# A two-layer decoder on one core: three single routed tiles share one buffer of three rows, with an empty step before their transposes, and three bias operations move behind Layer 0's last block

## The chip, the cores and the metric

The kernel runs on one core of a Trainium2 chip. The metric is the device time of one execution, in microseconds (us); the times given are the median of several runs. Beside them there is one profiled execution of each kernel, with a trace of every instruction; all line numbers (L208 and so on) are those of the kernel before, in its profile.

The engines are called TensorE (PE in the profile; PEld is its loading of weights), VectorE (DVE), ScalarE (ACT), GpSimd (POOL) and SyncE (SP). Each takes its instructions in the order of its own queue.

## The reference

Two decoder layers over x of shape (32, 100, 256), that is 3200 tokens of 256 numbers, with a context of shape (32, 361, 128). Cut to what matters:

```
x = x + L0_attn(layernorm(x))            # causal softmax attention, 16 heads of 64
x = x + L0_xattn(layernorm(x), ctx)      # cross attention to the context
x = x + L0_ffn(layernorm(x))             # 8 experts, top 2, and a shared expert
x = x + L1_attn(layernorm(x), W1, b1, W2, b2)   # linear attention scores, causal mask, 16 heads of 16
x = x + L1_xattn(layernorm(x), ctx)      # softmax cross attention, 16 heads of 64
x = x + L1_ffn(layernorm(x))             # 64 experts, top 8 in 4 of 8 groups, and a shared expert
```

The routing of the last stage, for each token:

```
scores = sigmoid(x @ gate_weight.T)
sfc = scores + e_bias
group_scores = sum of the two largest sfc in each of 8 groups of 8
keep the 4 best groups, then the 8 best experts of those
weights = scores of these 8, divided by their sum, times 2.5
expert e takes its tokens in order, at most 256
```

Everything is float32. The bias b1 of Layer 1's attention goes to the queries, the keys and the values.

## The kernel before

**Tiles and batches.** The 3200 tokens lie in SBUF as 25 tiles of 128 tokens (`x_sb`), numbered 0 to 24. Attention works by batches of 100 tokens, numbered 0 to 31, so a tile is complete when the batch that holds its last token is done. `tile_of(b)` says which tile batch b completes. Tiles 21, 22, 23 and 24 are completed by batches 28, 29, 30 and 31, one each.

**Who sets the order.** TensorE's order is written out by hand (`manual_schedule`): it follows the program. The other engines' orders are made by a scheduler, which takes operations as their inputs are expected to be ready, unless a dependency is added by hand (`self.depend`). A buffer with a tag rotates: with `bufs=2`, the third use waits until the first one's readers are done.

**Layer 0's experts.** `blocks0_run` runs 29 blocks in the order `ORDER0`: 24 of 256 rows and five of 128 rows ("half blocks"). In each, `block0` multiplies by the two hidden matrices (L155), ScalarE makes the silu (L1340) and VectorE the product `h` (L1341); then come the transposes of the next block's rows (L1299) and the products with the third matrix (L1362, L1368), which VectorE copies out (L1374). That copy is `self.late`. Behind each block, `behind` issues some of the small loads of Layer 1's weights and biases from a list (L1248), four of the small ones for a block; among them sixteen for the query biases (`wB<-in_bq`) and sixteen for the key biases (`wB<-in_bk`). Each block's own weights come by an indirect DMA of GpSimd (L1277).

**Layer 1's biases.** `l1_attn` puts three small operations on VectorE: two at L942 spread the query biases over two columns, and one at L943 copies the key biases. Their result `bias` is read by ScalarE when it evacuates queries and keys (L973, L970). In front of Layer 1's attention, L1266 adds the gathered expert rows to `x_sb`.

**Layer 1's cross attention with the routing beside it.** In `l1_xattn`, each batch has 13 steps. A step holds, on TensorE, the scores of one group of 128 query rows (L155), often one further matmul group, such as a part of the next batch's values projection (`vals1`), and the three transposes of an earlier group (L784). ScalarE makes the exponentials (L775, `wBx`) and copies the transposes (L785, `eT`); VectorE makes the maxima (L772) and scales the rows (L777). At the fourth step the values of the batch before are multiplied (L796).

When a tile is complete, `out` adds the projection to `x_sb` (L808 and L812) and takes the statistics for the norm. Its square root runs on ScalarE (L202), the reciprocal on VectorE (L205). The table `ROUTED` says which tiles are routed together: groups of three from tile 0 to 20, and then tiles 21, 22, 23 and 24 singly. `route` is a generator: at each `yield` it ends its part of the current step, and `tick` takes every open route on by one part at the end of each step. Its parts are: the normalised rows `xr` (L208), the transposes by TensorE (L230, evacuated by L149 or L150 in turn into `xnT`), the gate matmuls with the sigmoid (L1595), the choice of groups and experts on VectorE (L1598 to L1661), the places of the tokens with their experts (two matmuls, L1667 to L1677, giving `slot`), and eight sends for each tile: indirect DMAs of GpSimd (L1682), each of which writes 128 rows of `xr` to DRAM. There is at most one send in a step, and each waits for a piece of work of its step.

A row of `xr` is the 256 normalised numbers, the token's number (copied in by GpSimd, L1582) and 64 weights. Groups of three use the tag `xr`, with two buffers of three rows. Single tiles use the tag `xn`, with two buffers of two rows, of which one row is used:

```
if G == RG:
    xr = rp.tile([P, RG, XROW], F32, tag="xr", name="xr", bufs=2)
else:
    xr = self.lnp.tile([P, 2, XROW], F32, tag="xn", name="xr2")[:, :G]
```

**The end.** The last batch's steps, and the last tile's route, have parts of the shared expert between them (`shared1`, L1828, L1829 and L1836). When all sends have landed, GpSimd sets a flag, SyncE loads the first experts' rows, and `units` runs the experts of Layer 1, adding their results by indirect DMAs.

Of the kernel before, what the change touches and what calls it, by code (L numbers as in the profile page):

```python
# [9 lines left out]
F32 = mybir.dt.float32  # L10
# [3 lines left out]
ALU = mybir.AluOpType  # L14
AX = mybir.AxisListType

P = 128
# [3 lines left out]
NF = NT // P  # L21
# [23 lines left out]
XROW = D + 1 + E1  # L45

HALVES = {0: 6, 6: 6, 12: 6, 18: 7}
EDGES = {0: 6, 6: 6, 12: 6, 18: 3, 21: 2, 23: 2}
ROUTED = {**{f: 3 for f in range(0, 21, 3)}, **{f: 1 for f in range(21, NF)}}
FRONT0 = {**{f: 4 for f in range(0, 20, 4)}, 20: 5}  # L50
FRONT1 = {0: 4, **{f: 3 for f in range(4, NF, 3)}}
RG = 3
# [46 lines left out]
class Kernel:  # L99
# [619 lines left out]
    def l1_xattn(self):  # L719
        nc, tc, a = self.nc, self.tc, self.a  # L720
        self.route_begin()
        with ExitStack() as st:
# [80 lines left out]
            def out(f, part):  # L803
# [8 lines left out]
                nc.vector.tensor_tensor(self.x[:, f, :], self.po, self.x[:, f, :], ALU.add)  # L812
                self.norm_stats(f, ROUTED)
                for f0, n in ROUTED.items():
                    if f0 + n == f + 1 < NF:
# [105 lines left out]
    def l1_attn(self):  # L921
        nc, tc, a = self.nc, self.tc, self.a
        with ExitStack() as st:
            self.psum = st.enter_context(self.banks("l1a", t=8))
            wk, wq, wv, wo, bqk, bv, bo, xbo = self.w1a
# [11 lines left out]
            own = cp.tile([P, 2], F32, tag="own", name="own")  # L937
            nc.vector.tensor_single_scalar(own[:, 0:1], at, 0.0, op=ALU.is_equal)
            nc.vector.tensor_single_scalar(own[:, 1:2], at, 16.0, op=ALU.is_equal)
            bias = cp.tile([P, 3, 2], F32, tag="bias", name="bias")  # L940
            for j in range(2):
                nc.vector.tensor_scalar(bias[:, j, :], bqk[:, 0, :], own[:, j : j + 1], None, ALU.mult)  # L942
            nc.vector.tensor_copy(bias[:, 2, :], bqk[:, 2, :])  # L943
            vs = [cp.tile([T, H, 32], F32, tag=f"v{i}", name=f"v{i}") for i in range(3)]
            for v in vs:
                nc.gpsimd.memset(v, 0.0)
# [3 lines left out]
            def group(i):  # L950

                f = (0, 3 * i + 1)[i > 0]
                return range(f, f + FRONT1[f])
# [99 lines left out]
            with tc.manual_schedule(engines={mybir.EngineType.PE}):  # L1053
                for i in range(2):
# [9 lines left out]
                    f = group(i)[0]  # L1064
# [6 lines left out]
                for b in range(NB + 2):  # L1071
                    i = b % 4
# [497 lines left out]
    def route(self, f, G):  # L1570


        nc, tc, rp = self.nc, self.tc, self.rp
# [1 line left out]
        def t3(name, *shape, dt=F32):  # L1575
            return rp.tile([P, RG, *shape], dt, tag=name, name=name)[:, :G]

        if G == RG:
            xr = rp.tile([P, RG, XROW], F32, tag="xr", name="xr", bufs=2)
        else:  # L1580
            xr = self.lnp.tile([P, 2, XROW], F32, tag="xn", name="xr2")[:, :G]
        nc.gpsimd.tensor_copy(xr.bitcast(I32)[:, :, D], self.tok[:, f : f + G])  # L1582
        for j in range(G):
            self.norm_row(f + j, xr[:, j, :D], nc.vector)
            if j % 2 or j == G - 1:
                yield 1
        for j in range(0, G, 2):
            n = min(2, G - j)
            self.norm_turn(f + j, n, xr[:, j : j + n, :D], self.bank_t())
            yield 1  # L1590
# [88 lines left out]
        for j in range(G):  # L1679
            for k in range(TOPK):  # L1680
                yield SEND
                got = nc.gpsimd.indirect_dma_start(  # L1682
                    out=self.x1_d[:, :],
                    out_offset=bass.IndirectOffsetOnAxis(ap=slot[:, j, k : k + 1], axis=0),
                    in_=xr[:, j, :], in_offset=None,
                    bounds_check=E1 * CAP - 1, oob_is_err=False,
                )
# [63 lines left out]
    def l1_ffn(self):  # L1751
        nc, tc, a = self.nc, self.tc, self.a
        x = self.x
        with ExitStack() as st:
# [6 lines left out]
            with tc.manual_schedule(engines={mybir.EngineType.PE}):  # L1761
                next(steps)
                next(steps)

                (used, _), = self.routes
                next(used)
                next(route)
                us = next(steps)
                next(used)
                next(route)  # L1770
                us += next(steps)
                next(used)
                for _ in route:
                    pass
                while us < FIRST1:
                    us += next(steps)
# [309 lines left out]
```

## Time and profile before

| What | us |
|---|---|
| median of 3 runs | 2970.16 (2968.84 to 2970.37) |
| the profiled execution | 2999.12 |
| its span, first to last instruction | 2997.4 |
| TensorE busy in it | 2866.1 (96%) |
| VectorE busy | 1789.8 (60%) |
| ScalarE busy | 1415.9 (47%) |
| GpSimd busy | 914.0 (30%) |
| mean granted TensorE clock | 0.981 of full speed |
| Layer 0's blocks of experts | from about 1183 to 1592 |
| the last three batches' steps and values | from about 2684 to 2791 |
| the first load of experts' rows issued | 2830.9 |

The profiled execution is 1% longer than the median of the runs. A profile line of a group of instructions names line, engine, operation, output and inputs; brackets give the idle time of the engine just before it, and what ended that. The granted clock is a share of full speed: at 0.5 a matmul takes twice as long.

### The profile page before, as it was taken

To read this page: it belongs to the slowest core of one execution; us is meant where nothing else is said; L and a number is where in the kernel's file an instruction comes from. 1 tells how busy PE (TensorE), PEld (TensorE's weight loads), DVE (VectorE), ACT (ScalarE), POOL (GpSimd) and SP (SyncE) were. 2 spreads that over 40 slices of the span, in tenths; PEclk is the share of its full clock that TensorE was granted. 3 is DMA by queue.
4 is the path that set the end of the run, shared out by engine and by line. 5 is a ranking of instruction groups with operands and counts; after the bars stand their busy time and mean duration, and the time that the engine had idled before them with its cause. 6 is when DMAs were issued, how large, how long until landed. Compare 5 with 4: busy or idle time off the path is not lost. (4 is left out here: it accounts for less than half of the span.)

```text
span 2997.4 us, 66479 instructions
## 1 busy us (share of the span) xinstructions
PE 2866.1 (96%) x26012; PEld 2176.5 (73%) x26012; DVE 1789.8 (60%) x5120; ACT 1415.9 (47%) x4261; POOL 914.0 (30%) x1040
## 2 busy tenths in 40 slices
PE   8999999999999999999998999999999999998993
PEld 7777777677777756888885667777777777775672
DVE  6665666577777742222225778676666676776454
ACT  5554555567666631221223224565566566566220
POOL 3222221266655544100005431021311212123364
PEclk9999999999999989999998999999999999999997
DMA  9870000000000023654552100010000000000297
GB/s 316 272 276 1 1 1 1 14 15 16 15 15 15 8 87 122 211 202 183 199 217 74 32 2 10 6 42 20 26 11 12 12 12 11 12 10 5 83 229 194
DMA packets 127511, 224.12 MB, mean 75 GB/s; under 512 B 39470, under 2 KB 105446, under 8 KB 120401
## 3 DMA queue, kind: packets, MB, share of 16 engines
q1 hardware_dynamic: 97264, 125.64, 13.2%
q0 software_dynamic: 26640, 90.80, 9.3%
q8 instruction: 210, 3.44, 0.5%
q10 hardware_dynamic: 3280, 3.28, 0.3%
q14 instruction: 117, 0.95, 0.1%
HBM read 152.09 MB, written 112.56 MB: 88 GB/s over the span
## 5 line engine op out<-in xcount | busy, mean ns | idle before, releaser
L1682 POOL DMA_INDIRECT x_d<-xr,slot x200 | 195.5, 977 | 663.6 <-ACT eT L785 571.5
L155 PE MATMUL ps_t<-xnT,wA 128*128 128x200 f32 (+1 forms) x1608 | 329.9, 349 | 1.5 <-DMA wA<-in_wq 0.9
L155 PE MATMUL ps_t<-cT,q 128*128 128x361 f32 x832 | 317.4, 470 | 1.4 <-ACT wBx L775 1.4
L785 ACT COPY eT<-ps_t 124x384 f32<-124x384 f32 (+1 forms) x416 | 194.4, 476 | 229.7 <-PE ps_t L784 227.2
L775 ACT ACTIVATE wBx<-ps_t,m 128x361 f32<-128x361 f32 x416 | 236.7, 570 | 126.4 <-DVE m L772 118.6
L155 PEld LDWEIGHTS ps_t<-xnT,wA 128*128 128x128 f32 x1608 | 271.1, 191 | 32.4 <-issue 12.9
L534 DVE TENSOR_REDUCE m<-ps_t 100x1 f32<-100x361 f32 x512 | 239.6, 525 | 46.3 <-PE ps_t L155 46.1
L155 PE MATMUL ps_t<-xT,w 128*128 128x256 f32 (+1 forms) x1276 | 262.4, 365 | 0.7 <-ACT xT L149 0.7
L772 DVE TENSOR_REDUCE m<-ps_t 128x1 f32<-128x361 f32 x416 | 218.6, 527 | 60.8 <-PE ps_t L155 57.1
L155 PEld LDWEIGHTS ps_t<-xT,w 128*128 128x128 f32 x1276 | 225.1, 191 | 37.2 <-issue 9.6
L784 PEld LDWEIGHTS ps_t<-ident,wBx 128*124 128x124 f32 x1248 | 156.3, 140 | 123.1 <-issue 69.8
L357 POOL TENSOR_TENSOR e<-e,rz 100x400 f32<-100x400 f32 x128 | 109.5, 856 | 406.7 <-DVE rz L356 396.8
L556 ACT ACTIVATE e<-ps_t 121x300 f32<-121x300 f32 x512 | 173.9, 426 | 118.4 <-PE ps_t L155 118.3
L784 PE MATMUL ps_t<-ident,wBx 128*124 128x128 f32 x1248 | 204.7, 275 | 3.2 <-DVE sums L776 1.2
L353 ACT ACTIVATE e<-s,m 100x100 f32<-100x100 f32 x512 | 186.6, 368 | 21.2 <-DVE m L347 20.6
L155 PE MATMUL ps_t<-wA,cT 128*124 128x512 f32 x384 | 196.5, 600 | 0.0
L777 DVE TENSOR_SCALAR wBx<-wBx,sums 128x361 f32<-128x361 f32 x416 | 173.1, 416 | 9.9
L1341 DVE TENSOR_TENSOR h<-ps_t,g 128x256 f32<-128x256 f32 (+1 forms) x145 | 58.1, 402 | 186.1 <-ACT g L1340 186.1
L155 PEld LDWEIGHTS ps_t<-q,k 32*121 32x121 f32 x3072 | 128.0, 181 | 35.9 <-issue 11.3
L796 PEld LDWEIGHTS ps_t<-eT,v 124*64 124x64 f32 x3072 | 134.6, 137 | 23.1 <-issue 12.1
L796 PE MATMUL ps_t<-eT,v 124*64 124x100 f32 x3072 | 143.1, 250 | 4.9 <-issue 4.8
L1277 POOL DMA_INDIRECT w<-w_d,wid x29 | 29.6, 1019 | 376.0 <-PE ps_t L1368 343.7
(329 smaller groups left out, 5749.0 us busy)
## 6 DMA issues: line engine op xcount, KB each, us to landing
x_d<-fill SPq DMA_DIRECT2D x16, 1284.0 KB
we<-in_wexp SPq DMA_DIRECT2D x32, 384.0 KB
cT<-in_ctxT SPq DMA_DIRECT2D x64, 186.0 KB
xe_d<-zero SPq DMA_DIRECT2D x8, 1024.0 KB
xe<-x_d SPq DMA_DIRECT2D x24, 321.0 KB
sum<-fill SPq DMA_DIRECT2D x10, 640.0 KB
xe<-xe_d SPq DMA_DIRECT2D x24, 256.0 KB
y_d<-y SPq DMA_DIRECT2D x24, 256.0 KB
```

The source lines that it names most:

```text
L155: self.nc.tensor.matmul(out, lhsT=l, rhs=r, start=(i == 0), stop=(i == n - 1))
L353: nc.scalar.activation(t[:, i, :], s[:, i, :], AF.Exp, bias=m[:, i : i + 1], accum_out=rz[:, i : i + 1])
L357: nc.gpsimd.tensor_tensor(t[:, h, :], t[:, h, :], self.last(rz[:, h], T), ALU.mult)
L534: got = nc.vector.tensor_reduce(m[:, j, o : o + 1], ps[r], AX.X, ALU.max, negate=True)
L556: nc.scalar.activation(t[:, r], ps[r].rearrange("p (c t) -> p c t", c=NKC), AF.Exp)
L772: self.after = nc.vector.tensor_reduce(m, ps, AX.X, ALU.max, negate=True)
L775: nc.scalar.activation(t, ps, AF.Exp, bias=m, accum_out=z)
L777: nc.vector.tensor_scalar(t, t, z, None, ALU.mult)
L784: nc.tensor.transpose(pt[:, c, :], es[n % 5][:, c * KC : (c + 1) * KC], self.ident)
L785: self.after = nc.scalar.copy(eT[:, :, i * P : i * P + w], pt[:, :, :w])
L796: nc.tensor.matmul(pz[64 * j : 64 * j + 64, i, :], lhsT=v[:, c, h * 64 : (h + 1) * 64], rhs=eT[:, c, o : o + T], start=(c == 0), stop=(c = ...
L1682: got = nc.gpsimd.indirect_dma_start(out=self.x1_d[:, :], out_offset=bass.IndirectOffsetOnAxis(ap=slot[:, j, k : k + 1], axis=0), in_=xr[: ...
```

## The change

It does four things. Tiles 21, 22 and 23 take one buffer of the tag `xr` together, with a row each; tile 21 takes it out, tiles 22 and 23 use its second and third rows. Tile 24 goes on using the tag `xn`. In the routes of tiles 21, 22 and 23, a `yield` is added between the normalised row and the transposes, so that all that follows in these routes comes one step later. And the three bias operations of Layer 1 depend on `self.late`, which is the copy of Layer 0's last block by the time that `l1_attn` runs.

```diff
-ROUTED = {**{f: 3 for f in range(0, 21, 3)}, **{f: 1 for f in range(21, NF)}}
+SINGLE = 21
+ROUTED = {**{f: 3 for f in range(0, 21, 3)}, **{f: 1 for f in range(SINGLE, NF)}}
...
             for j in range(2):
-                nc.vector.tensor_scalar(bias[:, j, :], bqk[:, 0, :], own[:, j : j + 1], None, ALU.mult)
-            nc.vector.tensor_copy(bias[:, 2, :], bqk[:, 2, :])
+                got = nc.vector.tensor_scalar(bias[:, j, :], bqk[:, 0, :], own[:, j : j + 1], None, ALU.mult)
+                self.depend(got, [self.late.ins], "behind the last block")
+            got = nc.vector.tensor_copy(bias[:, 2, :], bqk[:, 2, :])
+            self.depend(got, [self.late.ins], "behind the last block")
...
-        if G == RG:
-            xr = rp.tile([P, RG, XROW], F32, tag="xr", name="xr", bufs=2)
+        i = (f - SINGLE) % RG
+        if f < SINGLE or i == 0 and f < NF - 1:
+            self.xr = xr = rp.tile([P, RG, XROW], F32, tag="xr", name="xr", bufs=2)
+            xr = xr[:, :G]
+        elif f < NF - 1:
+            xr = self.xr[:, i : i + 1]
         else:
             xr = self.lnp.tile([P, 2, XROW], F32, tag="xn", name="xr2")[:, :G]
         nc.gpsimd.tensor_copy(xr.bitcast(I32)[:, :, D], self.tok[:, f : f + G])
...
                 yield 1
+        if SINGLE <= f < NF - 1:
+            yield 1
         for j in range(0, G, 2):
             n = min(2, G - j)
             self.norm_turn(f + j, n, xr[:, j : j + n, :D], self.bank_t())
```

How the change moves the instructions on each engine, from the two kernels' programs: SyncE's sequence is the same. On TensorE the transposes, the gate matmuls and the matmuls of places of tiles 21 and 22, and the transposes and gate matmuls of tile 23, stand one step later. On VectorE the three bias operations stand behind Layer 0's last block, ahead of the first L1266, and the choice of experts of the three tiles is interleaved differently with the attention's work. On ScalarE the sigmoids of the three tiles, each with two table loads, stand one step later. On GpSimd the three copies of token numbers of tiles 21 to 23 stand together, ahead of the sends of tiles 18 to 20.

## The prediction

> **What bounds the kernel now.** I read the page first, then the waits of TensorE by stretches, then the timeline of each engine around every wait that an edit touches. The page says that TensorE sets the time:
>
> ```profile
> PE 2866.1 (96%) x26012; PEld 2176.5 (73%) x26012; DVE 1789.8 (60%) x5120; ACT 1415.9 (47%) x4261; POOL 914.0 (30%) x1040
> ```
>
> With TensorE at 96%, a gain can only come from a place where TensorE itself stands idle, or runs at a lower granted clock. The waits of TensorE (who waited for whom: us in total, times, longest) name the places. First those of 1130 to 1620 us, Layer 0's blocks of experts; then those of 2600 to 2840 us, the last batches of Layer 1's cross attention:
>
> ```profile
> PE ps_t L1362 <- DVE h L1341: 2.9, 1, 2.9
> ...
> PE ps_t L230 <- DVE xr L208: 9.7, 4, 4.7
> ```
>
> The first is behind the biases. VectorE's timeline (start, length, in brackets the idle time before it and what ended it):
>
> ```profile
> 1404.91 0.36 DVE L942 TENSOR_SCALAR bias<-wB,own 128x2 f32<-128x2 f32 x2 [5.12 <-DMA xe<-xe_d]
> ...
> 1464.82 0.17 DVE L943 COPY bias<-wB 128x2 f32<-128x2 f32 x1 [4.94 <-DMA wB<-in_bk]
> ```
>
> Two tiny operations of Layer 1, put by the scheduler into the middle of Layer 0's blocks, hold VectorE for 5 us each until their small loads land. Behind the first queue the products h (L1341) of a block that is half as wide as the others, so that TensorE runs out of work; behind the second they queue too, but that block is a whole one, and TensorE shows no idle time there. What the first costs, TensorE's busy time and granted clock (PEclk) over the stretch from this half block's start to the end of the next block's first products, and over the same stretch of the next half block:
>
> ```profile
> 1395.32:1419.58 24.26, 21.40 (x107) 0.86 0.57 212
> 1485.17:1503.10 17.93, 17.93 (x106) 1.00 0.86 294
> ```
>
> 24.26 - 17.93 = 6.33 us for the same matmuls: 2.86 idle, the rest a clock of 0.86 behind the gap.
>
> The second place is the routing of tiles 21, 22 and 23, one tile each. TensorE's timeline at their transposes:
>
> ```profile
> 2699.59 0.44 PE L230 MATMUL ps_t<-ident,xr 128*128 128x128 f32 x2 [1.63 <-DVE xr L208]
> ...
> 2732.77 0.41 PE L230 MATMUL ps_t<-ident,xr 128*128 128x128 f32 x2 [2.88 <-DVE xr L208]
> ...
> 2770.77 0.66 PE L230 MATMUL ps_t<-ident,xr 128*128 128x128 f32 x2 [4.70 <-DVE xr L208]
> ```
>
> And what the normalised row (L208) itself waited for, on VectorE, at tiles 22 (its reciprocal) and 23:
>
> ```profile
> 2732.01 0.16 DVE L205 RECIPROCAL rstd<-rstd 128x1 f32<-128x1 f32 x1 [1.76 <-ACT rstd L202]
> ...
> 2770.21 0.41 DVE L208 TENSOR_SCALAR xr<-x_sb,mv,rstd 128x256 f32<-128x256 f32 x1 [2.08 <-DMA x_d<-xr,slot]
> ```
>
> Two different causes. Tiles 21 and 22 wait for the chain of statistics, ScalarE's square root (table load 1.28, root 0.20) and the row. Tile 23 waits for its buffer: the tag xn has two, tile 21 holds one, and tile 21's last send leaves at 2768.06 and lands at 2770.1.
>
> **The edits, one by one.**
>
> *Biases.* The three operations (0.36 for the two at L942, 0.17 at L943) move behind the last block's copy on VectorE. The wait they carry is for loads issued by 1458 us and landed by 1464.2, so it is over. There they stand ahead of the gathers' sums (L1266):
>
> ```profile
> 1598.84 0.48 DVE L1266 SCALAR_TENSOR_TENSOR x_sb<-yk,wA,x_sb 128x256 f32<-128x256 f32 x1 [6.64 <-DMA yk<-y_d,wA]
> ```
>
> 6.64 us of idle VectorE take 0.5 us of work: cost nothing; without that cover, 0.5 us. Their first reader is an activation at 1622. No DMA is moved: SyncE's sequence is the same. Gain 6.33; if the gap were there but not the slow clock, 2.86. Below that I see no bound, as the other half blocks show what is late next: nothing, they run at 17.93.
>
> *One buffer of three rows.* Tile 21 takes the buffer that tiles 15 to 17 used. Their last send left at 2646.78 and tile 21's row is written at 2699.13, so that wait is over by far. The sequences of both kernels show the row writes of tiles 22 and 23 with no wait on a DMA any more: different rows of one tile. The three copies of token numbers (0.18 each, L1582) go ahead in GpSimd's queue to where it idles 23.76 us before 2671.52; behind them queue sends that wait for later work anyway. Two waits of 1.21 us for a landing, in GpSimd's queue ahead of sends, fall away; GpSimd is idle 12.25 us before the last tile's sends, so this is nothing.
>
> *The empty step.* Transposes, gate matmuls and the sigmoid of tiles 21 to 23 come one step later, one step being scores, at times a values projection, and three transposes. No matmul is added. One evacuation each changes engine: tile 21's goes to ScalarE (0.36), tile 22's to VectorE. Here ScalarE decides, since it has to switch tables around each sigmoid:
>
> ```profile
> 2737.21 1.28 ACT L1595 ACT_TABLE_LOAD   x1
> 2738.50 0.23 ACT L1595 ACTIVATE sc<-ps_t 128x64 f32<-128x64 f32 x1
> 2738.74 1.28 ACT L775 ACT_TABLE_LOAD   x1
> ```
>
> That is 2.8 us in which no exponential is made. The Trainium skill, ScalarE: Activation LUTs, section What ACT_TABLE_LOAD costs, adds a drain of about 1.38 us to each load. By it the pair would take an estimated 5.6 us with the sigmoid, which speaks against putting it later; the trace has the sigmoid 0.01 us behind its load, and the measurement decides.
>
> Tile 21: TensorE is freed of 1.63 us. ScalarE, which had waited 2.41 for the projection behind that stall, is then busy without a gap from 2701.53 to 2712.7, where the batch's values begin. So the values come earlier by what ScalarE starts earlier, 1.63 and the transposes' 0.28, less the copy of 0.36: 1.5. Ends: 0, if the sigmoid's place eats it, and 3.9, all of TensorE's gaps here (1.63 + 1.42 + 0.88).
>
> Tile 22: the row is ready at 2732.62. With one step more (0.61 + 0.86 + 0.33 = 1.8) the transposes would wait about 1.1 instead of 2.88, and the clock stays up. TensorE would win 1.8 and the 1.8 of slow clock (scores 1.25 for 0.77, projection 1.91 for 1.02, transposes 0.85 for 0.49). But ScalarE is busy from the square root on, with gaps of only 0.67 and 0.48, and gives up 0.36: 1.5. Ends 0 and 3.6.
>
> Tile 23: without the buffer the row can be written at 2765.7, right behind its reciprocal; the transposes, a step later, are at about 2767.1 and wait for nothing. TensorE wins the 4.70 and the slow clock behind it:
>
> ```profile
> 2766.00:2770.70 4.70, 0.07 (x1) 0.00 (x0) 1.10 (x2) 3.05 (x4) 1.16 (x2) 1.00 0.01 0
> 2770.70:2775.60 4.90, 4.83 (x19) 3.71 (x20) 1.68 (x5) 2.33 (x5) 0.99 (x1) 0.65 0.00 0
> ```
>
> 4.90 x (1 - 0.65) = 1.7, together 6.4. ScalarE here had 4.16 us idle until 2773.24, then 1.61 later, 5.8 in all; its chain of two table switches, silu and three copies can move up by that. I take 5.8, the smaller; ends 4.0 and 6.4. Tile 23's choice of experts on VectorE (2776.24 to 2783.2) must be over before the matmul of places at 2791.41; that slack shrinks from 8 to about 5 us, which still holds. The last tile's route, its sends, the flag and the experts' first rows all follow TensorE's end of the values, so they move as a block.
>
> Sum: 6.33 + 1.5 + 1.5 + 5.8 = 15.1 us; ends 2.9 + 0 + 0 + 4.0 = 6.9 and 6.3 + 3.9 + 3.6 + 6.4 = 20.2. The profiled execution took 2999.12 us (span 2997.4 and 1.7 around it), 1% over the median of 2970.16. So 2984.0 for a profiled one; the gain scaled by 0.99 is 15, and the median 2955.
>
> On the clock, the Trainium skill, TensorE: Matmul & The Clock Gate, section What's actually happening, lets the clock halve after one idle window of about 3.4 us. By it the gaps of 2.86 and 2.88 would often leave it up, and the sum would be some 3.5 us less, by the biases' slow stretch; here both were followed by slow matmuls, the gap of 1.63 was not.
>
> **Rivals.**
> 1. *ScalarE and VectorE keep what TensorE gives at tiles 21 and 22, and undisturbed runs lose no clock at the biases.* For it: ScalarE has hardly a gap there, and the biases' gap of 2.86 is the shortest that cost clock. Against: the other half blocks run clean. 2.9 + 0 + 0 + 4.0 to 5.8 = 7 to 9 us: about 2962. Chance 0.15. The rule on the clock in the Trainium skill (TensorE: Matmul & The Clock Gate, What's actually happening) is on this rival's side.
> 2. *Slower: the sigmoid's two loads, one step later, meet steps with nothing but scores and transposes.* Then scores want banks that no exponential has freed, and TensorE stands for the 2.8 of the pair and, past a gap of about 2.9, loses 1.8 of clock. Three tiles of 4.6 are 13.8; if that replaces the gains, less 6.3 of the biases, 7.5 slower: 2978. It decides only if a gap reaches 2.9 at all three. For it: gaps of 1.42 and 0.88 already follow tile 21's sigmoid. Against: groups of three, whose sigmoid comes five steps behind the start, show no wait after theirs (2646 to 2650). Chance 0.04. The drain that the Trainium skill gives (ScalarE: Activation LUTs, What ACT_TABLE_LOAD costs) would make it likelier; the trace shows none.
> 3. *No change that can be told (within 0.2%, 6 us):* as 2, but at one or two tiles, or both gaps weaker without the profiler. 2967. Chance 0.08.
> 4. *The row of tile 22 would wait for tile 21's sends, as one tile is shared.* The landing at 2770 would then hold work of 2732, some 38 us. The sequences show no such wait: left out.
>
> **How the numbers follow.** The forecast, 0.73, is 2955, with 2950 to 2960 its own range. The range asked for goes up to rival 1's time and a little on for the bounds, and down to the 20 us end: 2948 to 2965. A measurement of this kernel tells about 0.2% from no change. Faster by more than that: forecast and nearly all of rival 1, 0.87; the same 0.09; slower 0.04.
>
> **What would show it.** In the profile after: L942 and L943 next to the gathers at 1590, and the fourth half block's stretch at 17.9; no DMA as releaser of tile 23's L208; L230's waits of 2600 to 2840 down from 9.7 to about 1.5; the batch values behind tile 23 some 15 us earlier than 2784. The forecast is wrong if TensorE shows new gaps, released by ScalarE, behind the three sigmoids that add up to over 6 us, or if the experts' rows at the end do not move with the values.

## The result, and the profile after

| | kernel before | kernel after |
|---|---|---|
| median of the runs, us | 2970.37 (2968.84 to 2976.96) | 2955.06 (2951.76 to 2959.07) |
| ratio, 95% interval | | 0.9945 (0.9933 to 0.9957) |
| the profiled execution, us | 2999.12 | 2956.08 |

By the ratio the change gains 16.3 us, 12.8 to 19.9 by its interval; the two medians differ by 15.3. The profiled execution of before is no measure of the gain: the same kernel, profiled once more in the first experiment, had a span of 2971.1 us in place of 2997.4. From here on "before" in a comparison of traces is that second profile, unless the first is named.

The page of after, TensorE's busy time, and its waits of 1130 to 1620 us, where the line for h is gone and only waits of the start of Layer 1 are left, the two longest of which are:

```profile
PE 2851.3 (97%) x26012; PEld 2172.6 (74%) x26012; DVE 1787.6 (61%) x5120; ACT 1412.4 (48%) x4261; POOL 913.0 (31%) x1040
```

```profile
PE ps_t L704 <- PEq L1255: 3.8, 1, 3.8
PE ps_t L231 <- DVE xn L209: 2.9, 1, 2.9
```

The three bias operations on VectorE in the trace of after (their lines are now L943 and L945), and the half block that they had held up, over the stretch that the prediction took:

```profile
1588.17 0.36 DVE L943 TENSOR_SCALAR bias<-wB,own 128x2 f32<-128x2 f32 x2 [1.36 <-DVEq L1255]
1588.44 0.16 DVE L945 COPY bias<-wB 128x2 f32<-128x2 f32 x1
1593.19 0.48 DVE L1269 SCALAR_TENSOR_TENSOR x_sb<-yk,wA,x_sb 128x256 f32<-128x256 f32 x1 [4.60 <-DMA yk<-y_d,wA]
```

```profile
1396.25:1414.18 17.93, 17.93 (x106) 15.88 (x105) 4.82 (x14) 4.41 (x13) 2.00 (x2) 1.00 0.77 287
```

They stand ahead of the gathers' sums and inside VectorE's idle time. The half block runs without a gap at full clock, in the 17.93 us that the other half blocks take.

TensorE's waits of 2550 to 2820 us and, from its timeline, the transposes of tiles 21, 22 and 23 (L231) with the two new waits between them:

```profile
PE ps_t L785 <- DVE m L1627: 2.1, 1, 2.1
PE ps_t L785 <- DVE cnt L1625: 1.5, 1, 1.5
PE ps_t L231 <- DVE xr L209: 1.4, 2, 1.1
```

```profile
2672.25 0.41 PE L231 MATMUL ps_t<-ident,xr 128*128 128x128 f32 x2
2681.00 0.52 PE L785 MATMUL ps_t<-ident,wBx 128*124 128x128 f32 x3 [1.45 <-DVE cnt L1625]
2702.38 0.41 PE L231 MATMUL ps_t<-ident,xr 128*128 128x128 f32 x2 [1.08 <-DVE xr L209]
2710.88 0.55 PE L785 MATMUL ps_t<-ident,wBx 128*124 128x128 f32 x3 [2.06 <-DVE m L1627]
2735.22 0.38 PE L231 MATMUL ps_t<-ident,xr 128*128 128x128 f32 x2
```

The row waits fell from 9.7 to 1.4 us, tile 23's 4.70 to nothing. In their place stand two waits of L785, the attention's own transposes, 1.45 us behind tile 21's sigmoid and 2.06 behind tile 22's. The releasers named are small operations of the choice of experts, on VectorE.

To compare kernels I take **tile stretches**: the time on TensorE from the start of the values (L796 before, L797 after) of one batch to those of the next. Tile 21's ends with batch 29's values, tile 22's with batch 30's, tile 23's with batch 31's. This needs no common clock, and it holds each tile's whole gain or loss.

| kernel, us | tile 21 | tile 22 | tile 23 | sum |
|---|---|---|---|---|
| before | 34.13 | 31.78 | 38.41 | 104.32 |
| buffer only | 34.31 | 31.86 | 32.26 | 98.43 |
| step only | 31.98 | 29.87 | 37.37 | 99.22 |
| buffer and step | 31.98 | 30.91 | 32.84 | 95.73 |
| after (biases too) | 31.96 | 31.12 | 32.65 | 95.73 |
| after, step for tiles 21 and 22 only | 31.98 | 31.28 | 32.19 | 95.45 |
| after, exponential for the sigmoid | 30.32 | 27.87 | 32.25 | 90.44 |

Behind tile 23, the time from the start of the last tile's matmuls of places to the first transposes of experts' rows is the same in before and after, 21.88 us, so what the tiles give is kept. It can differ by itself: four other traces take some 23.5 us there, one of a kernel whose routing is that of before (key_bias_only) among them.

### The profile page after: what moved, and what is told of

The parts are those of the page before. It is cut to its first block, busy times and chain, and to the rows that moved or that the text cites. A ratio compares the mean times of both kernels' runs of the same rounds, so it can differ in the third digit from the quotient of the medians.

```text
span 2954.3 us, 66469 instructions
## 1 busy us (share of the span) xinstructions
PE 2851.3 (97%) x26012; PEld 2172.6 (74%) x26012; DVE 1787.6 (61%) x5120; ACT 1412.4 (48%) x4261; POOL 913.0 (31%) x1040
## 5 line engine op out<-in xcount | busy, mean ns | idle before, releaser
L785 PEld LDWEIGHTS ps_t<-ident,wBx 128*124 128x124 f32 x1248 | 156.1, 139 | 123.4 <-issue 68.2
L785 PE MATMUL ps_t<-ident,wBx 128*124 128x128 f32 x1248 | 203.9, 275 | 5.3 <-DVE m L1627 2.1
L797 PEld LDWEIGHTS ps_t<-eT,v 124*64 124x64 f32 x3072 | 133.1, 137 | 16.4 <-ACT wBx L776 5.6
L1343 ACT ACTIVATE g<-ps_t 128x256 f32<-128x256 f32 (+1 forms) x145 | 52.9, 365 | 190.9 <-PE ps_t L156 190.9
## 6 DMA issues: line engine op xcount, KB each, us to landing
xe_d<-zero SPq DMA_DIRECT2D x8, 1024.0 KB, 16.3
```

The lines of the kernel that those rows point to most:

```text
L785: nc.tensor.transpose(pt[:, c, :], es[n % 5][:, c * KC : (c + 1) * KC], self.ident)
L797: nc.tensor.matmul(pz[64 * j : 64 * j + 64, i, :], lhsT=v[:, c, h * 64 : (h + 1) * 64], rhs=eT[:, c, o : o + T], start=(c == 0), stop=(c = ...
```

## The experiments

**The kernel before once more (before_again).** 

> The kernel before, unchanged, for a second profiled execution. The profiled one shown took 2999.12 us, 29 above the median, and lay 17 us behind the changed kernel's between 1600 and 1720 us (start of Layer 1's attention, granted clock 0.74 to 0.91 there against 0.99 to 1.00). Theory 1, that stretch has nothing to do with the change: this profile takes 2965 to 2975 and shows a clock of 0.97 or more in most of that stretch; the waits of 2.9 (half block) and 1.6, 2.9, 4.7 (tiles 21 to 23) are there again. Theory 2, the change mends that stretch too: the low clock is there again and the profile is again near 2999.

Measured: ratio 1.0001 (0.9991 to 1.0010), span 2971.1, and the four waits are there again, as Theory 1 says. The first profile's extra 26 us lie for the most part at the start of Layer 1's attention (229.8 us from the first L703 to the first score, here 214.1), where VectorE and GpSimd meet (last section). The prediction's scaling by 0.99 took only 0.1 us off its sum. But the places of the change were longer in the first profile too: 1.24 us at the half block, 0.70 at tile 22 and 0.84 at tile 23.

**The biases alone (bias_only).** The edit is the change's second hunk without the rest.

> Only the three bias operations go behind Layer 0's last block. Forecast's theory: 6.3 us faster, ratio 0.9979; the stretch of the fourth half block and the next block's first products takes 17.9 instead of 24.3. Rival (undisturbed runs lose no clock there): 2.9 us faster, ratio 0.9990. Rival (the start of Layer 1's attention is mended by the moved operations): over 10 us faster, ratio below 0.9966.

Measured: 0.9977 (0.9968 to 0.9986), 6.8 us, as the forecast's theory has it; the ratios of both rivals lie outside the interval. From the half block's first transposes (L1299) to the next block's, TensorE takes 18.01 us in before and 12.91 here, so 5.10 of it lie there. The stretch of the prediction, in before and here:

```profile
1394.27:1417.29 23.02, 19.91 (x107) 16.84 (x106) 5.09 (x16) 4.42 (x13) 2.00 (x2) 0.93 0.60 223
```

```profile
1393.53:1411.46 17.93, 17.93 (x106) 15.88 (x105) 4.82 (x14) 4.42 (x13) 2.01 (x2) 1.00 0.76 287
```

Waits of 2.80 and 0.30 and the slow clock behind them are gone. The time from the half block's transposes to the next block's is not the same in each trace of a kernel with the wait: 18.00, 18.01, 18.09 and 18.17 in four of them, 19.25 in the first profile of before and 19.64 in one below. The longer gap is 2.8 to 3.0 in all of them; what differs most is how long the slow clock lasts. So the gain there is 5.1 to 6.7.

**Buffer and step, without the biases (route_only).** The edit is the change's other hunks.

> Only the routing part: one buffer of three rows and the empty step, the biases as before. Forecast's theory: 8.8 us faster (1.5, 1.5 and 5.8 at tiles 21, 22 and 23), ratio 0.9970; the wait of 2.9 at the half block is still there. Rival (ScalarE and VectorE keep the gains at tiles 21 and 22): 4 to 6 us, ratio 0.9980 to 0.9987.

Measured: 0.9975 (0.9965 to 0.9984), 7.4 us; the half block's wait of 2.8 is still there. By the time alone the rival's 6 us would fit too; the stretches, 8.6 us in all, speak for the forecast's 8.8, though not for its split over tiles 21 and 22. With the biases' 6.8 it makes 14.2, against 16.3 for both: the parts add up within their intervals.

**The buffer without the step (buffer_only).**

```diff
-        if SINGLE <= f < NF - 1:
-            yield 1
```

(out of the version with buffer and step)

> Only the buffer of three rows, without the empty step, the biases as before. Forecast's theory: tile 23's row is written at its reciprocal and its transposes wait about 0.7 us instead of 4.7, tiles 21 and 22 wait 1.6 and 2.9 as before: 5.5 us faster, ratio 0.9981. Rival (without the step the square root on ScalarE, its table load and the row still hold the transposes for over 2.5 us): 2 us faster, ratio 0.9993.

Measured: 0.9977 (0.9967 to 0.9987), 6.8 us; the rival's 2 us lie outside the interval. Its waits of TensorE, 2550 to 2830 us:

```profile
PE ps_t L231 <- DVE xr L209: 5.2, 4, 2.9
PE ps_t L156 <- ACT wBx L776: 1.4, 1, 1.4
```

Tile 23's stretch falls by 6.15 us with the buffer alone, tiles 21 and 22 keep their waits and their times. The buffer is all that tile 23 needs.

**The step without the buffer (step_only).**

```diff
+        if 21 <= f < NF - 1:
+            yield 1
```

(into the kernel before)

> The kernel before with the empty step alone: the biases stay in Layer 0's blocks, and single tiles keep their two old buffers. Theory 1 (the step is what helps tiles 21 and 22, the buffer what helps tile 23): tile 21's stretch, from its batch's values to the next, is shorter by 2.15 us and tile 22's by 0.8, as in the run with buffer and step; tile 23's row still waits for the landing of tile 21's last send, and the step covers only some 1.4 of its 4.7 us, so 1 to 3 us there. Sum 4 to 6 us, ratio 0.998 to 0.9987 against the kernel before. Theory 2 (the step gains nothing without the buffer): tile 21 and 22 as before, ratio 0.9995 to 1.0005.

Measured: 0.9986 (0.9977 to 0.9994), 4.2 us; the stretches give 2.15, 1.91 and 1.04, 5.10 in all. Tile 23's wait is still there, shorter by less than a step:

```profile
2741.02 0.69 PE L230 MATMUL ps_t<-ident,xr 128*128 128x128 f32 x2 [3.82 <-DVE xr L208]
```

Theory 2 is out: the step works without the buffer. With the buffer there, it adds 98.43 - 95.73 = 2.70 us.

**The key biases alone (key_bias_only).** Only L943's copy depends on `self.late`, the two operations at L942 stay.

> The kernel before with only the copy of the key biases (L943) behind Layer 0's last block; the two operations at L942 stay. Theory 1 (only the wait behind a half block costs time): TensorE had no idle time at L943's wait, so the half block's wait of 2.8 us stays and the ratio is 0.9995 to 1.0005. Theory 2 (the gain of about 1.9 us at the start of Layer 1's attention, seen with all three operations moved, hangs on which operations VectorE has there): that part comes with L943 alone, the reciprocal square root (L201) takes 0.23 us and not 1.8, and the ratio is about 0.9993. Theory 3 (both waits cost about the same): 2.5 us or more, ratio 0.999 or less.

Measured: 0.9998 (0.9989 to 1.0007). The half block's wait stays:

```profile
PE ps_t L1363 <- DVE h L1342: 3.0, 1, 3.0
```

VectorE's wait of nearly 5 us behind a whole block cost TensorE nothing: from that block's transposes to the next it takes 15.08 us in before, with the wait, and 15.09 here, without it. The 5.12 behind a half block cost 5 to 7. Theory 3 is out.

Theory 2 stays open. I had seen the start of Layer 1's attention take some 2 us less in the two traces with moved biases and suspected a link. Its signs came here: L201 is short (0.22 us), and that part takes 212.2 us from the first L703 to the first score, as with all three operations moved (212.1), against 214.1 in before. Its 2 us lie inside the interval of the time, so the time can't decide. In the step-only kernel, with the biases where they were, that part is as fast (211.8), so it can be fast without them; but with the buffer only and with buffer and step, the biases in place too, it takes 214.2 and 214.3.

**No table to switch at the gates (exp_gates).** On the kernel after:

```diff
-        nc.scalar.activation(sc, pr, AF.Sigmoid)
+        nc.scalar.activation(sc, pr, AF.Exp, scale=-1.0)
+        nc.vector.tensor_scalar_add(sc, sc, 1.0)
+        nc.vector.reciprocal(sc, sc)
```

> The changed kernel with the gates' sigmoid written as an exponential of -x on ScalarE, and +1 and a reciprocal on VectorE, so that ScalarE has no table to switch at any gate. Theory 1 (ScalarE's two table loads around the sigmoid cause the new waits of 1.45 and 2.06 us behind the sigmoids of tiles 21 and 22, and hold their gains down): the two waits go, tile 22's stretch falls from 31.1 to 29 or 30 us, tile 21's from 32.0 to 30 or 31, 3 to 4 us faster than the changed kernel, ratio 0.993 to 0.9935 against the kernel before. Theory 2 (the choice of experts on VectorE causes them, as the releasers named say): both waits stay or grow by the two operations added, stretches within 0.3 of 32.0 and 31.1, ratio 0.994 to 0.9955. The earlier tiles' sigmoids may give something under either theory, so the stretches decide.

Measured: 0.9933 (0.9919 to 0.9946). Both L785 waits are gone, though VectorE has two more operations in the very chain that was named as the releaser. TensorE at the transposes of the three tiles:

```profile
2671.32 0.41 PE L231 MATMUL ps_t<-ident,xr 128*128 128x128 f32 x2
2699.80 0.41 PE L231 MATMUL ps_t<-ident,xr 128*128 128x128 f32 x2 [1.08 <-DVE xr L209]
2729.00 0.38 PE L231 MATMUL ps_t<-ident,xr 128*128 128x128 f32 x2
```

Tile 21's stretch falls by 1.64 us, little more than its wait of 1.45, tile 22's by 3.25, which is more than its 2.06. The rest is clock. Three stretches in after, one up to the end of that wait and two behind it (TensorE's busy time comes second, the granted clock is the third number from the end):

```profile
2705.50:2710.88 5.38, 3.32 (x19) 2.21 (x18) 4.41 (x19) 5.32 (x10) 2.04 (x3) 1.00 0.01 0
2710.88:2713.78 2.90, 2.90 (x8) 1.37 (x8) 2.38 (x15) 2.86 (x11) 2.29 (x3) 0.56 0.10 28
2713.78:2716.80 3.02, 3.02 (x61) 3.02 (x62) 2.48 (x12) 0.77 (x4) 0.53 (x1) 0.86 0.05 14
```

2.90 x 0.44 + 3.02 x 0.14 = 1.7 us lost to the clock, with the 2.06 some 3.7. The last of the three begins with the values and so lies in tile 23's stretch; tiles 22 and 23 together fall by 3.65. The cause can be followed on ScalarE's timeline of after:

```profile
2706.37 1.28 ACT L1604 ACT_TABLE_LOAD   x1
2707.67 0.22 ACT L1604 ACTIVATE sc<-ps_t 128x64 f32<-128x64 f32 x1
2707.91 1.28 ACT L776 ACT_TABLE_LOAD   x1
```

The next exponential can start at 2709.2; its row is scaled by VectorE at 2710.33 and transposed at 2710.88. VectorE's choice of experts fills the time just before that, and so the view names it; without the loads the wait is gone and the choice of experts is still there. Theory 1 is shown; its size was forecast too small, 3 to 4 us against 5.3 by the stretches. (The loads of the other tiles' gates are gone too; the stretches show what those of 21 to 23 cost.)

**The step for tiles 21 and 22 only (step_two_tiles).** `if SINGLE <= f < NF - 2` in place of `NF - 1`.

> The changed kernel with the empty step for tiles 21 and 22 only; tile 23 has the shared buffer without the step. Theory 1 (the buffer alone takes tile 23's wait away): tile 23's stretch is 32.3 us, as with the buffer alone, against 32.65 with the step, so 0 to 0.5 us faster than the changed kernel, ratio 0.9938 to 0.995 against the kernel before. Theory 2 (tile 23 needs the step too, once tiles 21 and 22 run earlier): a wait of 1 to 3 us comes back at its transposes (L231), stretch 33.5 to 36 us, ratio 0.995 to 0.996.

Measured: 0.9938 (0.9924 to 0.9952), no wait at tile 23's transposes, its stretch 32.19 against 32.65. The time can't tell 0.5 us; the trace says that the step at tile 23 gains nothing.

**Four together.** These four ran beside one another on another chip, on which the kernel before takes 2999.85 us, so they are compared among themselves.

After (after_again): 

> The changed kernel once more, beside the next three, so that they are compared in the same runs. All theories: ratio 0.9935 to 0.9955 against the kernel before; stretches of tiles 21, 22 and 23 of 32.0, 31.1 and 32.65 us.

Exponentials (exp_gates_again): 

> The changed kernel with exponentials for the sigmoids, once more beside the changed kernel. If the two table loads are the cause, it is 4 to 5 us faster than the changed kernel in the same runs, stretches 30.3, 27.9 and 32.25 us; if its profile was a lucky one, less than 2 us.

Exponentials, step for two tiles (exp_two_tiles): 

> Exponentials for the sigmoids, and the empty step for tiles 21 and 22 only. Theory 1 (at tile 23 the buffer is all that is needed): tile 23's stretch is 32.2 us or a little less, and the time within 1 us of the version with the step at all three. Theory 2 (without a sigmoid's loads behind it, the step at tile 23 hides the chain of the norm): a wait of 1 us or more at tile 23's transposes, and 1 to 2 us slower.

Exponentials, no step (exp_no_step): 

> Exponentials for the sigmoids, the shared buffer and the moved biases, without any empty step. Theory 1 (the step's worth is the chain of statistics, square root and row that it hides, whatever the gate's tables cost): the waits of 1.6 and 2.9 us at the transposes of tiles 21 and 22 come back, stretches of about 32 and 30 us in place of 30.3 and 27.9, 3 to 4.5 us slower than with the step. Theory 2 (the tables were the cause of the row's waits too, because they delayed ScalarE's square root): the waits at the transposes are under 1 us without a step, and the time is within 1.5 us of the version with it.

| kernel | median, us | ratio (interval) | tile 21 | tile 22 | tile 23 | sum |
|---|---|---|---|---|---|---|
| after | 2986.28 | 0.9944 (0.9925 to 0.9964) | 31.97 | 30.61 | 33.52 | 96.10 |
| exponentials | 2982.21 | 0.9935 (0.9916 to 0.9954) | 30.32 | 28.05 | 32.95 | 91.32 |
| exponentials, step for two tiles | 2982.90 | 0.9938 (0.9919 to 0.9957) | 30.33 | 28.11 | 32.61 | 91.05 |
| exponentials, no step | 2984.89 | 0.9941 (0.9922 to 0.9960) | 31.50 | 31.87 | 32.54 | 95.91 |

The stretches repeat to within 0.9 us: the exponentials give 4.8 us here and 5.3 on the other chip. By the medians it is 4.1; the intervals overlap, so the timing alone would not tell it. Without the step the waits at the transposes come back, 1.81 at tile 21 and 2.88 at tile 22, and the three stretches are 4.6 us longer: the step hides statistics, root and row, and is worth more (4.6 against 2.70) when no table load stands behind it. Theory 1 of that run holds: 3 to 4.5 us were expected, the stretches give 4.6 and the medians 2.7; tile 22's 31.87 is longer than the 30 expected. With the step for two tiles, tile 23's transposes wait for nothing and the median is 0.7 us from that with three steps, as Theory 1 of that run says; tile 23's stretch is 32.61, not 32.2. By its medians the version with exponentials is the fastest of all tried, though not beyond the intervals.

## Why the prediction was right, point by point

**The time.** 2955 was forecast, and 2955.06 measured. That they agree to 0.1 us is luck: three of its four terms were off, not all to one side, and over the whole span the traces of before and after differ by 16.8 us, of which the places that it counted hold 13.7 (5.1 and 8.6). The other 3 lie elsewhere: after is behind by 2.0 before the half block, and gains 2.0 at the start of Layer 1's attention and some 3.4 in the last experts' units. The units, from the first experts' transposes to TensorE's last matmul, take 118.5 to 122.2 us in the ten traces ahead of the last four, though no edit touches them; whether the 2.0 at the start of Layer 1's attention hang on the moved operations stays open.

**Biases: right, at the upper end.** The step "24.26 - 17.93 = 6.33" is exact for the trace that it was read from (after: 17.93). Five further traces with the wait give 5.1, 5.1, 5.2, 5.3 and 6.7. The trace that was read showed a tail of slow clock that is shorter in four of these five. The claims that L943's wait costs nothing and that the moved operations cost nothing were both right.

**Tile 21: mechanism right, 1.5 forecast, 2.17 measured.** The row's wait went, as forecast. ScalarE's gaps were the wrong end to count from: the pair of loads, a step later, brought a wait of 1.45 where 1.42 and 0.88 had stood in the old trace. With it came a wait of 0.64 for the evacuation that ScalarE now makes, and still the sigmoid's place cost TensorE a little less than before.

**Tile 22: the step that failed in its size.** 1.5 forecast, 0.66 measured (1.36 against the first profile, which had 32.48). The forecast had the row's wait at 1.1, and it is 1.08. Of TensorE's 3.6 it left 2.1 with ScalarE, as that engine is busy and gets one copy more; in fact the two loads made one gap of 2.06 with a slow clock behind it, 3.7 us, which is the mechanism of rival 2 at one tile of three. Without the loads tile 22 gives 31.78 - 27.87 = 3.91: a little over the upper end of 3.6. How much is left varies with the clock: three other traces with this gap and a slow clock behind it give 0.5 to 1.2, and the step-only trace, where the clock stayed up behind the same gap, gives 1.91.

**Tile 23: right.** 5.8 forecast, 5.76 measured, 6.15 by the buffer alone. Against the first profile, from which the forecast was read, it is 6.60, a little above its end of 6.4. No DMA releases the row, and the reciprocal goes straight into it:

```profile
2733.60 0.16 DVE L206 RECIPROCAL rstd<-rstd 128x1 f32<-128x1 f32 x1 [0.91 <-ACT rstd L203]
2733.80 0.41 DVE L209 TENSOR_SCALAR xr<-x_sb,mv,rstd 128x256 f32<-128x256 f32 x1
```

Sum of the three tiles: 8.8 forecast, 8.59 measured. "Some 15 us earlier" for the values behind tile 23 is 13.87 against the second trace of before (2760.30 and 2746.43); the 2784 of the first held time that it had lost ahead of this. The new gaps behind the sigmoids, 1.45 and 2.06, add up to 3.5, under the 6 that would have made the forecast wrong.

**"Here ScalarE decides": right,** and shown by taking its loads away, against the releasers named in the view.

**The clock.** "The gap of 1.63 was not" followed by slow matmuls holds, and 1.45 was not either; but the 2.8 that the forecast used is not the least gap with a slow clock behind it: 2.06 was followed by 0.56. Nor is such a gap always followed by it. TensorE behind it in after, and in the step-only kernel:

```profile
2711.24 2.61 PE L156 MATMUL ps_t<-cT,q 128*128 128x361 f32 x4
```

```profile
2714.33 0.52 PE L784 MATMUL ps_t<-ident,wBx 128*124 128x128 f32 x3 [2.05 <-DVE m L1620]
2714.68 1.38 PE L155 MATMUL ps_t<-cT,q 128*128 128x361 f32 x4
```

The same four scores take 2.61 and 1.38 us; in the second the granted clock stays at 1.00. Of five traces with this gap, four show the slow clock behind it. The Trainium skill, TensorE: Matmul & The Clock Gate, What's actually happening, gives one idle window of about 3.4 us, free-running, as the condition. The gaps of 2.06 and of 2.80 to 2.98 are shorter, and the slow clock came; the traces decide, and by them a gap of 2 us can be enough.

**The rivals.** 1 fell: the second trace of before and four more lost clock at the half block, and tiles 21 and 22 gave 2.8 together, not 0. 2 fell as a whole, as no gap behind a sigmoid reached 2.9, but its mechanism cost 3.25 of the 3.91 us that tile 22 had to give. The drain of about 1.38 us that the Trainium skill adds to each table load (ScalarE: Activation LUTs, What ACT_TABLE_LOAD costs) is not in the traces: the load starts 0.02 us behind the copy ahead of it, and the sigmoid 0.02 us behind its load. 3 fell with the measured ratio, 4 with the trace of after, which has no wait for a send at tile 22's row.

## What to carry to other kernels

A tiny operation that waits for a load costs what is queued behind it at that moment: the same 5 us of waiting on VectorE cost 5 to 7 us behind a half block and nothing that shows behind a whole one, so look at who stands idle, not at the wait. When a wait is taken from the engine that sets the time, ask what its other suppliers do in the next two microseconds: here a pair of table loads became the next wait, and rewriting the sigmoid with the exponential that is loaded anyway gave 5 us more by the traces. The releaser that a view names is the last to come; take the suspected cause away before you believe it or its neighbour.

## What the runs showed of the hardware

**VectorE is held up beside GpSimd's adds.** At the start of Layer 1's attention GpSimd adds a bias to three tiles (L223). In the second trace of before, a 128x3 operation of VectorE that elsewhere takes 0.17 us ran into it (the first line is VectorE's, the second GpSimd's):

```profile
1637.16 1.78 DVE L201 TENSOR_SCALAR rstd<-mv 128x3 f32<-128x3 f32 x1
```

```profile
1636.82 2.09 POOL L223 TENSOR_TENSOR x_sb<-x_sb,wB 128x256 f32<-128x256 f32 x3
```

It ends at 1638.94, GpSimd at 1638.91, and TensorE waits 1.77 us for what VectorE does next. In the trace with the biases alone GpSimd's three adds are over by 1632.75, ahead of that L201, which starts at 1632.88 and takes 0.23. On the chip of the last four runs, three sums of VectorE (L1269) that take 1.31 us in the first trace of after ran beside GpSimd's adds (1620.74 to 1622.83) and took longer in the same way:

```profile
1619.84 3.68 DVE L1269 SCALAR_TENSOR_TENSOR x_sb<-yk,wA,x_sb 128x256 f32<-128x256 f32 x3
```

The Trainium skill, SBUF — State Buffer, Who interferes with whom, says that the two share a pair of ports which one of them holds for a whole instruction while the other stops, and that the order of issue decides who stops. In the traces VectorE stands beside GpSimd's adds as this says, here through all three of them and not only one. The stretch from the first L704 to the first score took 229.5 us in that trace of after and 212.1 in the first. Such stops may be what makes this part of the kernel vary from trace to trace and from chip to chip, but that is not shown: the trace of exp_gates_again has the three sums at 1.28 us and takes longest there, 233.1. What sets the order, and how much of the 17 us these stops explain, was not tried.
